# A shorter life for the activations by token, the attention residual as a matrix product, and 1,056 more columns for the attention's ring

## The chip, the cores and the metric

The kernel runs on one core of a Trainium2 chip. The metric is the device time of one execution in microseconds. All data is float32 unless a line says otherwise; a "column" below is one float32 on each of 128 partitions.

## The reference, cut to what matters

Eight residual layers with a layer norm behind each run over 4 sequences of 1,024 tokens of width 128: an attention by similarity, a binarised feed-forward, an attention among the 64 channels of each of 16 heads, a ternary feed-forward, a gated linear recurrence, four experts, a state-space layer, and a product-key mixture with the two best of 64 experts. The part that the change touches most is the third:

```python
x = _layernorm(x + _L1_attn_ref(x, ...))
# inside, for every token and head, Q, K and V of 64 values each:
scores = einsum('bshq,bshk->bshqk', Q, K)      # 64 x 64 per token and head
scores = where(triu(ones(C, C), 1), -inf, scores)
w = softmax(scores)
attn = einsum('bshqk,bshk->bshq', w, V)        # then reshaped and @ Wo
```

Each score is a product of two numbers, so the work is elementwise: exp(q*k - m) for every pair below the diagonal.

## The kernel before, in words

**Order.** The program is written out by a planner in Python. Every piece of work is a generator that yields the engine it needs next and the buffers that must be free; `Order.run` picks the step that can start first by the planner's own estimates, with ranks between steps that could start together. The planner thus fixes one order of instructions for each engine and for the DMA queue of SP; the chip then only waits on semaphores.

**Blocks and chains.** The 32 tiles of 128 tokens form 8 blocks of four tiles. Each block goes through a front (`layer0`, `layer1`), then through the channel attention tile by tile (`prepare`, `feed`, `rest`, `invert`, `close`), then through chain a (`layer3` to `layer5`), chain b (`layer6`) and chain c (`layer7`). The last block goes through the three chains as two groups of two tiles. The chains of older blocks are placed between the attention work of newer ones; when the attention has ended, only the chains of the last groups remain.

**The attention's pieces.** A unit is 64 tokens (half a tile), so there are 64 units. Each is cut into 17 pieces in a fixed order: a diagonal piece of 1,024 columns, seven pieces of 896, 768, 640, 512, 384, 256 and 128, a second diagonal piece of 1,024, and eight pieces of 1,920, 1,792, 1,664, 1,536, 1,408, 1,280, 1,152 and 1,024: 17,408 columns. A piece goes through six steps: VectorE multiplies q by k into the ring (GpSimd does so for the pieces of 896 and 1,536), GpSimd subtracts the maximum, ScalarE takes the exponential, TensorE adds up the denominator (`den`), VectorE multiplies by v, TensorE adds up the numerator (`num`). Then the piece's room is given back.

**The ring.** All pieces live in one buffer of `ERING` columns, handed out in order. A piece that does not fit between the head and the end starts again at column 0; what is left at the end stays unused in that lap. A piece can start only when the older pieces in its room have been through the numerator:

```python
def at(self, n):
    start = self.head if self.head + n <= self.size else 0
    for a, b in self.held:
        if start < b and a < start + n:
            return None
    if self.held and start < self.head:
        if any(a >= self.head for a, b in self.held):
            return None
    return start
```

After the last piece the ring is cut into pieces of 512 columns that join the buffer tags `b` and `c` of the last chains.

**Activations by token and transposed.** A block has `x` (tokens on partitions) and `xT` (features on partitions), five buffers of 512 columns for each. `x` is loaded or made in the front and kept until `layer7` writes it to DRAM (`xs`) as its first step. `close` ends a tile's attention: the product with `Wo`, an addition of `x` on VectorE (line 1053), the norm on ScalarE into `x`, a transpose into `xT`. After the front one row of `xT` (feature 96) is overwritten by ones, to carry biases; since the activations have a mean of zero over the features, that feature is minus the sum of the others. The other layers add their residual already as a product of `xT` with the identity. `layer5` adds the experts up in `x`.

Of the kernel before, what the change touches and what calls it, by code (L numbers as in the profile page):

```python
# [15 lines left out]
ALU = mybir.AluOpType  # L16
# [4 lines left out]
P = 128  # L21
NB, SEQ, D = 4, 1024, 128
NG = 8
TPG = 4
# [4 lines left out]
BIG = 3.0e38  # L29
H, C, R, S, NK = 16, 64, 4, 2, 16  # L30
SH = S * H
ERING = 8904
LUMPS = 4
EPS = 0.05
SLACK = {}
# [2 lines left out]
    "ident": P, "a0_W1": 1, "a0_b1": 1, "f0_b1": 4, "f1_lnw": 4, "f1_lnb": 4, "a2_nw": 1, "f2_b1": 16, "f2_Wu": 1,  # L38
    "f2_bu": 1, "a3_bdt": 16, "a3_Alog": 16, "f3_sup": 1, "f3_sdn": 1, "bup": 64, "bdn": 32, "rep": 32, "SL": P, "U": P,
    "ex4": P, "ex2": P, "g4": 16, "g2": 32, "su": P, "sd": P, "par": 4, "iota": LUMPS, "blk": P, "bz": 48,  # L40
    "route": 16, "beyond": R,
}
ONE = 96
LAG = {"chain_a": (0.7, 300), "chain_b": (1.6, 290), "chain_c": (2.6, 132)}
# [275 lines left out]
class Model:  # L320
# [4 lines left out]
    def __init__(self, ctx, tc, a):  # L325
        self.tc, self.nc, self.a = tc, tc.nc, a
        self.n = 0
        self.sb = ctx.enter_context(tc.tile_pool(name="sb", bufs=1))
        self.ps = ctx.enter_context(tc.tile_pool(name="ps", bufs=1, space=PSUM))
        self.dram = ctx.enter_context(tc.tile_pool(name="scratch", bufs=1, space=DRAM))  # L330
        self.order = Order(URGE, HOP)
        nc = self.nc
        self.pe, self.v, self.s, self.g, self.d = (
            (Tensor if n == "PE" else Engine)(self.order, e, n)
            for e, n in ((nc.tensor, "PE"), (nc.vector, "DVE"), (nc.scalar, "ACT"), (nc.gpsimd, "POOL"), (nc.sync, "SP"))
        )

        self.room = {
# [3 lines left out]
            "den": (1, 512), "num": (1, 512), "kvr": (2, 512), "bg": (4, 512),  # L342
        }

        self.held, self.most = 0, 2
        self.slots, self.tags, self.users = {}, {}, {}
        for tag, (n, cols) in self.room.items():
            pool = self.ps if tag in ("den", "num", "kvr", "bg") else self.sb
            self.slots[tag] = [self.keep([P, cols], tag, pool=pool) for _ in range(n)]
            for t in self.slots[tag]:  # L350
                self.tags[self.order.owner(t)] = tag, t
# [211 lines left out]
        for j in range(n):  # L563
            self.s.activation(x[:, j, :], r[:, j, :], AF.Copy, scale=rs[:, j : j + 1])

    def norm(self, g, c, r):

        x, rs = g.x, self.small([P, TPG], c + "rs")[:, : g.n]
        yield "ACT"
        self.level(x, r, rs)  # L570
        self.drop(r)
        yield from self.transpose(g.xT, [x[:, j, :] for j in range(g.n)])

    def own(self, g):

# [22 lines left out]
    def normalise(self, g, nT):  # L598
        sq = self.small([P, TPG], "sq")
        rn = self.small([P, TPG], "rn")  # L600
        yield "ACT", self.free("a")
        nrm = self.new("a", TPG, D)
        for j in range(TPG):
            self.s.activation(nrm[:, j, :], g.x[:, j, :], AF.Square, accum_out=sq[:, j : j + 1])
        yield "POOL"
        self.g.tensor_scalar_max(sq, sq, 1e-12)
        self.g.tensor_tensor(rn, sq, self.neghalf, ALU.pow)
        yield "ACT"
        for j in range(TPG):
            self.s.activation(nrm[:, j, :], g.x[:, j, :], AF.Copy, scale=rn[:, j : j + 1])  # L610
        yield from self.transpose(nT[:, (g.k % 2) * GT : (g.k % 2) * GT + GT], [nrm[:, j, :] for j in range(TPG)])
        self.drop(nrm)
        yield from self.transpose(g.xT, [g.x[:, j, :] for j in range(TPG)])

    def similar(self, nT, i, h, out):
        yield "PE", self.free("bg")
# [35 lines left out]
    def layer0(self, b):  # L652

        room = "ha" if b else "hc"
        gs = self.blocks[2 * b : 2 * b + 2]
        for g in gs:
            if g.x is None:
                yield "SP", self.free("x")
                self.load_x(g.k)
            yield "ACT", self.free("xT")  # L660
            g.xT = self.new("xT")
        yield "ACT", self.free(room)
        nT = self.new(room)
        yield from self.together(*(self.normalise(g, nT) for g in gs))
        if b == 0:
            yield from self.count(gs[0], nT)
            return nT
        yield from self.together(*(self.count(g, nT) for g in gs))
        self.drop(nT)
# [348 lines left out]
    def close(self, unit):  # L1018

        T, u = unit["T"], unit["u"]  # L1020
        g, j = divmod(T, TPG)
        yield "DVE", self.when(lambda: "a" in unit, lambda: self.order.until(unit["a"]))
        a, num, aT = unit["a"], unit["num"], self.aT
        self.v.tensor_tensor(a, num.rearrange("p h c -> p (h c)"), a, ALU.mult)
        self.drop(num)
        if unit is self.units[-1]:
            self.retire("num", "bg")
            self.most = 4

        yield "PE", self.free("bg", also=lambda: self.closed == 2 * T + u)  # L1030
        ps = self.new("bg", 4, P)
        for i in range(4):
            self.pe.transpose(ps[:, i, :], a[:, i * P : (i + 1) * P], self.ident)
        self.drop(a)
        yield "ACT"
        self.s.copy(
            aT.rearrange("p (b c) t -> p c b t", b=2)[:, :, :, 64 * u : 64 * u + 64],
            ps.rearrange("p c (b t) -> p c b t", b=2),
        )
        self.drop(ps)  # L1040
        if u == 1:
            yield "PE", self.free("bg")
            po = self.new("bg")[:, :D]
            self.bias_row(po, 1, D, first=D)
            for i in range(8):
                if i == 4:
                    yield "PE"
                self.pe.matmul(po, lhsT=aT[:, i, :], rhs=self.Wo[:, i, :], start=False, stop=(i == 7))
            self.closed += 1
            yield "DVE"  # L1050
            x = self.blocks[g].x[:, j, :]
            rs = self.small([P, 1], "crs")
            self.v.tensor_tensor(po, x, po, ALU.add)
            yield "ACT"
            self.level(x[:, None, :], po[:, None, :], rs)
            yield "PE"
            self.pe.transpose(po, x, self.ident)
            yield "ACT"
            self.s.copy(self.blocks[g].xT[:, j * P : (j + 1) * P], po)
            self.drop(po)  # L1060
            self.normed += 1
        else:
            self.closed += 1
# [83 lines left out]
    def layer4(self, g):  # L1147
        a, xT, n = self.a, g.xT, g.n
# [13 lines left out]
        q, k, f, gate = (big[:, i, :] for i in range(4))  # L1162
# [88 lines left out]
            self.pe.matmul(po[:, j, :], lhsT=og[:, j * P : (j + 1) * P], rhs=Wo, start=True, stop=False)  # L1251
            self.pe.matmul(po[:, j, :], lhsT=xT[:, j * P : (j + 1) * P], rhs=self.ident, start=False, stop=True)
        self.drop(big, og, sq, Wo)
        yield from self.norm(g, self.own(g), po)


    def layer5(self, g):
# [83 lines left out]
    def layer6(self, g):  # L1341
# [223 lines left out]
            self.pe.matmul(po[:, j, :], lhsT=drained[j // 2][:, 0, j % 2, :], rhs=Wout, start=True, stop=False)  # L1565
            self.pe.matmul(po[:, j, :], lhsT=xT[:, j * P : (j + 1) * P], rhs=self.ident, start=False, stop=True)
        self.drop(room, w, *drained, *(() if n == TPG else (dx,)))
        yield from self.norm(g, "b", po)


    def top2(self, c, pl, Q, used, expand, places, n, spread):
# [102 lines left out]

    def layer7(self, g):
        a, k, n = self.a, self.k, g.n
        xs, ys = (self.keep([n * P, D], name, pool=self.dram) for name in ("xs", "ys"))
        yield "SP"
        self.d.dma_start(xs.rearrange("(j p) d -> p j d", p=P), g.x)
        self.drop(g.x)  # L1680
        Wup = yield from self.load("c", a["f3_Wup"].rearrange("p (s e) -> p s e", e=64), 8, 64)
        yield "SP", self.free("c")
        xq = self.new("c", 4 * n, 32)
# [183 lines left out]
    def chain_a(self):  # L1867
# [14 lines left out]
        for g in self.groups:  # L1882
            b = self.blocks[g.t0 // TPG]

            yield "PE", self.when(lambda: self.done5 >= g.k - (g.k == len(self.groups) - 1))

            for k in {0: (2, 3), 1: ()}.get(g.k, range(b.k + 2, min(b.k + 3, NG)) if g.t0 % TPG == 0 else ()):
                yield from self.front(self.blocks[k])
            yield "PE", self.when(lambda: self.normed >= g.t0 + g.n, lambda: self.order.until(b.xT))
            if g.t0 % TPG == 0:  # L1890
                self.users[b.x.tensor.name] = self.users[b.xT.tensor.name] = sum(
                    o.t0 // TPG == b.k for o in self.groups
                )
            if g.n < TPG:
                self.order.split(b.x, 256)
                self.order.split(b.xT, 256)
            j = g.t0 % TPG
            g.x, g.xT = b.x[:, j : j + g.n, :], b.xT[:, j * P : (j + g.n) * P]
            self.order.spawn(one(g), "chain_a", self.order.latest)

    def chain_b(self):
# [70 lines left out]
def arrays_of(i):  # L1972
    f = {k: np.asarray(v) for k, v in i.items()}
    c = np.ascontiguousarray
# [64 lines left out]
    for n, s in (("up", "up"), ("dn", "down")):  # L2039
# [16 lines left out]
        "g4": p // 4 == np.arange(16)[None, :],  # L2056
        "g2": p % 32 == np.arange(32)[None, :],
        "beyond": (p // 32 > np.arange(R)[None, :]) * -BIG,
        "su": (p % 4 == q % 4) & (p // 4 == q // 8),
        "sd": (p % 32 == q // 4) & (p // 32 == q % 2),  # L2060
        "par": np.concatenate([p // n % 2 == np.arange(2)[None, :] for n in (4, 2)], 1) * LUMPS,
# [25 lines left out]
```

## Time and profile before

| | us |
|---|---|
| median of 3 runs (lowest, highest) | 3816.46 (3814.92, 3824.07) |
| the profiled execution, its own time | 3811.2 |
| its span, first to last instruction | 3809.4 |
| TensorE busy | 3041.4 (80%) |
| VectorE busy | 3163.6 (83%) |
| ScalarE busy | 2498.4 (66%) |
| GpSimd busy | 2815.1 (74%) |
| mean granted TensorE clock | 0.922 |

In the profile PE is TensorE's matmuls, PEld its weight loads, DVE is VectorE, ACT ScalarE, POOL GpSimd and SP the engine that issues the DMAs. All helpers share one recorded line (L60), so groups are told apart by the names of their buffers: `ringe` is the ring, `qr` and `kvr` hold queries and keys with values, `mr` the maxima, `den` and `num` are the sums in PSUM, `bg` are general PSUM banks. A group's row gives the busy time and the mean ns of one instruction, then the idle time of that engine just before these instructions and what ended it. A row of waits gives the total us, the number of waits and the longest.

### The profile page before, as it was taken

How to read it: one execution, taken by the hardware profiler on the slowest of the kernel's cores; microseconds unless marked ns; L12 is line 12 of the kernel's file. 1: busy time of each engine (PE TensorE's matmuls, PEld its weight loads, DVE VectorE, ACT ScalarE, POOL GpSimd, SP SyncE). 2: the span in 40 equal slices, each digit the busy share in tenths (PEclk: the TensorE clock that was granted, in tenths of full speed). 3: DMA queues.
4: the chain of work that ended last, by engine and by line, in shares of the span. 5: the costliest groups of instructions: out<-in, count | busy, mean ns of one | idle time of the engine just before them, and what ended most of it. 6: DMA issues, size and time to landing. Idle time of an engine off the chain costs nothing.

```text
span 3809.4 us, 130461 instructions
## 1 busy us (share of the span) xinstructions
PE 3041.4 (80%) x56496; PEld 1616.4 (42%) x56496; DVE 3163.6 (83%) x3988; ACT 2498.4 (66%) x5206; POOL 2815.1 (74%) x1320
## 2 busy tenths in 40 slices
PE   5567667877778888988888987988888887879873
PEld 2224232433334543544444543544444443446652
DVE  2888999999899889999899789899998999983321
ACT  4557565667757885777657885777666775666641
POOL 0778997899879887898878887798887997970000
PEclk8889889989999999999999998999999999989886
DMA  2332221312214334243433433343432334523564
GB/s 70 77 80 52 45 53 45 88 45 54 49 49 107 91 79 110 67 120 85 106 82 88 105 83 83 89 123 79 109 94 73 93 85 104 141 80 100 162 158 104
DMA packets 374135, 334.04 MB, mean 88 GB/s; under 512 B 196332, under 2 KB 304172, under 8 KB 373560
## 3 DMA queue, kind: packets, MB, share of 16 engines
q1 hardware_dynamic: 364216, 292.15, 30.8%
q0 software_dynamic: 9344, 33.56, 2.9%
q8 instruction: 442, 7.24, 0.8%
q14 instruction: 133, 1.09, 0.1%
HBM read 149.16 MB, written 42.21 MB: 50 GB/s over the span
## 4 chain that ended last, share of the span: by engine, by line
PE 26%; DVE 21%; ACT 13%; POOL 8%; issue 8%; DMA 3%; SPq 1%; DVEq 0%; ACTq 0%; POOLq 0%
PE bg L60 15%; DVE ringe L60 14%; POOL ringe L60 8%; ACT ringe L60 5%; PE den L60 5%; PE num L60 4%; DVE bg L60 4%; PE kvr L60 2%; ACT b L60 2%; ACT ha L60 1%; ACT x L60 1%; SPq L60 1%; ACT L60 1%; ACT t L60 1%; DVE a L60 0%
## 5 line engine op out<-in xcount | busy, mean ns | idle before, releaser
L60 POOL TENSOR_TENSOR ringe<-ringe,mr 128x1024 f32<-128x1024 f32 (+14 forms) x1088 | 2450.2, 2289 | 436.2 <-DVE ringe L60 331.7
L60 DVE TENSOR_TENSOR ringe<-ringe,kvr 128x1024 f32<-128x1024 f32 (+14 forms) x1097 | 1290.8, 1206 | 149.9 <-PE den L60 132.6
L60 ACT ACTIVATE ringe<-ringe 128x768 f32<-128x768 f32 (+14 forms) x962 | 1001.2, 1057 | 528.8 <-POOL ringe L60 525.1
L60 DVE TENSOR_TENSOR ringe<-qr,kvr 128x1024 f32<-128x1024 f32 (+12 forms) x960 | 1110.0, 1192 | 52.1 <-PE num L60 32.6
L60 PE MATMUL num<-ringe,cst 128*32 128x256 f32 (+7 forms) x8728 | 692.1, 405 | 247.4 <-DVE ringe L60 239.9
L60 PE MATMUL den<-ringe,cst 128*32 128x256 f32 (+7 forms) x8728 | 679.1, 408 | 184.7 <-ACT ringe L60 160.8
L60 PEld LDWEIGHTS num<-ringe,cst 128*32 128x32 f32 x8728 | 220.5, 112 | 566.8 <-DVE ringe L60 457.1
L60 PEld LDWEIGHTS den<-ringe,cst 128*32 128x32 f32 x8728 | 237.4, 113 | 464.4 <-ACT ringe L60 248.7
L60 POOL TENSOR_TENSOR ringe<-qr,ks 128x896 f32<-128x896 f32 (+1 forms) x128 | 287.7, 2248 | 74.7 <-PE num L60 34.7
L60 PE MATMUL bg<-xT,a 128*32 128x512 f32 (+1 forms) x1880 | 248.5, 621 | 37.4 <-DVE bg L60 11.7
L60 ACT ACTIVATE ringe<-ringe,cst 128x256 f32<-128x256 f32 x512 | 217.8, 500 | 65.0 <-POOL ringe L60 64.7
L60 DVE TENSOR_TENSOR_SCAN bg<-ends,bg 128x512 f32<-128x512 bf16 x128 | 155.3, 1218 | 37.9 <-PE bg L60 37.1
L60 PE MATMUL kvr<-wkv,xT 128*32 128x256 f32 x2048 | 150.5, 415 | 27.3 <-DVE ringe L60 26.7
L60 PE MATMUL bg<-a,ha 128*32 128x128 f32 x4608 | 154.9, 276 | 11.5 <-ACT ha L60 11.5
L60 ACT COPY b<-bg 128x512 f32<-128x512 f32 (+2 forms) x214 | 95.6, 453 | 69.7 <-PE bg L60 68.2
L60 PEld LDWEIGHTS bg<-a,ha 128*32 128x32 f32 x4608 | 123.8, 112 | 32.7 <-issue 15.1
L60 ACT ACTIVATE ha<-bg,cst 128x512 f32<-128x512 f32 (+1 forms) x155 | 100.0, 674 | 56.4 <-PE bg L60 56.1
L60 PE MATMUL bg<-xT,b 128*32 128x128 f32 (+1 forms) x3528 | 127.2, 285 | 2.7 <-ACT last L60 0.9
L60 ACT ACTIVATE b<-cst,little 128x128 f32<-128x128 f32 x392 | 124.7, 399 | 0.0
L60 PEld LDWEIGHTS bg<-xT,a 128*32 128x32 f32 x1880 | 58.4, 116 | 140.4 <-issue 60.7
L60 PEld LDWEIGHTS bg<-xT,b 128*32 128x32 f32 x3528 | 102.3, 114 | 33.4 <-issue 16.9
L60 PE MATMUL bg<-b,cst 128*32 128x512 f32 x832 | 109.8, 600 | 4.6 <-ACT b L60 4.6
(678 smaller groups left out, 4431.3 us busy)
## 6 DMA issues: line engine op xcount, KB each, us to landing
qr<-q SPq DMA_DIRECT2D x512, 128.0 KB
mr<-t SPq DMA_DIRECT2D x512, 128.0 KB
c<-in_f_Wdn SPq DMA_DIRECT2D x55, 256.0 KB
c<-tu SPq DMA_DIRECT2D x204, 64.0 KB
tu<-gt SPq DMA_DIRECT2D x25, 512.0 KB
td<-gt SPq DMA_DIRECT2D x24, 512.0 KB
c<-td SPq DMA_DIRECT2D x94, 128.0 KB
a<-in_f_W SPq DMA_DIRECT2D x36, 256.0 KB
```

The costliest lines, as they stand in the source:

```text
L60: return f(*args, **kw)
```

## The change

`x` lives only inside norms, and from `layer4`'s norm to the end of `layer5`; three buffers of 512 columns serve instead of five. `normalise` drops `x` after its transposes, `norm` takes a buffer of its own and drops it again, `layer6` writes `xs` to DRAM itself as soon as its norm is done (before, `layer7` did that first). In `close` the addition on VectorE goes; instead TensorE adds the product of `xT` with a constant `more` (the identity, with column 96 made of -1 and row 96 of 0) into the same PSUM bank ahead of the products with `Wo`, and the norm writes into a small buffer `cx`. `TensorE` matmuls of this kind are issued as four, of 32 columns of the stationary operand each. The constants grow by 128 columns, `cx` takes 128, and the ring has 9,960 columns instead of 8,904.

```diff
-ERING = 8904
+ERING = 9960
...
-    "route": 16, "beyond": R,
+    "route": 16, "beyond": R, "more": P,
...
-            "x": (5, 512), "xT": (5, 512), "a": (6, 512), "b": (12, 512), "c": (4, 512), "gt": (1, 1024), "xp": (2, 152),
+            "x": (3, 512), "xT": (5, 512), "a": (6, 512), "b": (12, 512), "c": (4, 512), "gt": (1, 1024), "xp": (2, 152),
...
-    def norm(self, g, c, r):
-
-        x, rs = g.x, self.small([P, TPG], c + "rs")[:, : g.n]
-        yield "ACT"
-        self.level(x, r, rs)
+    def norm(self, g, c, r, keep=False):
+
+        rs = self.small([P, TPG], c + "rs")[:, : g.n]
+        if g.x is None:
+            yield "ACT", self.free("x")
+            g.x = self.new("x", g.n, D)
+        else:
+            yield "ACT"
+        self.level(g.x, r, rs)
         self.drop(r)
-        yield from self.transpose(g.xT, [x[:, j, :] for j in range(g.n)])
+        yield from self.transpose(g.xT, [g.x[:, j, :] for j in range(g.n)])
+        if not keep:
+            self.drop(g.x)
+            g.x = None
...
         yield from self.transpose(g.xT, [g.x[:, j, :] for j in range(TPG)])
+        self.drop(g.x)
+        g.x = None
...
             self.bias_row(po, 1, D, first=D)
+            self.pe.matmul(
+                po, lhsT=self.blocks[g].xT[:, j * P : (j + 1) * P], rhs=self.k["more"], start=False, stop=False
+            )
             for i in range(8):
...
-            yield "DVE"
-            x = self.blocks[g].x[:, j, :]
-            rs = self.small([P, 1], "crs")
-            self.v.tensor_tensor(po, x, po, ALU.add)
+            rs, x = self.small([P, 1], "crs"), self.small([P, D], "cx", bufs=1)
             yield "ACT"
             self.level(x[:, None, :], po[:, None, :], rs)
...
-        yield from self.norm(g, self.own(g), po)
+        yield from self.norm(g, self.own(g), po, keep=True)
...
-        yield from self.norm(g, "b", po)
+        yield from self.norm(g, "b", po, keep=True)
+        yield "SP"
+        g.xs = self.keep([n * P, D], "xs", pool=self.dram)
+        self.d.dma_start(g.xs.rearrange("(j p) d -> p j d", p=P), g.x)
+        self.drop(g.x)
...
-        xs, ys = (self.keep([n * P, D], name, pool=self.dram) for name in ("xs", "ys"))
-        yield "SP"
-        self.d.dma_start(xs.rearrange("(j p) d -> p j d", p=P), g.x)
-        self.drop(g.x)
+        xs, ys = g.xs, self.keep([n * P, D], "ys", pool=self.dram)
...
+        "more": ((p == q) * 1.0 - (q == ONE)) * (p != ONE),
```

More of the change, by code (lines that the diff above doesn't have):

```diff
@@ L656, in layer0 @@
         for g in gs:
-            if g.x is None:
+            if g.k > 1:
                 yield "SP", self.free("x")
@@ L1890, in chain_a @@
             if g.t0 % TPG == 0:
-                self.users[b.x.tensor.name] = self.users[b.xT.tensor.name] = sum(
-                    o.t0 // TPG == b.k for o in self.groups
-                )
+                self.users[b.xT.tensor.name] = sum(o.t0 // TPG == b.k for o in self.groups)
             if g.n < TPG:
-                self.order.split(b.x, 256)
                 self.order.split(b.xT, 256)
             j = g.t0 % TPG
-            g.x, g.xT = b.x[:, j : j + g.n, :], b.xT[:, j * P : (j + g.n) * P]
+            g.xT = b.xT[:, j * P : (j + g.n) * P]
             self.order.spawn(one(g), "chain_a", self.order.latest)
```

## The prediction

> **What bounds the kernel now.** I read the page's busy shares first, then the busy time by stages, then the waits of VectorE and GpSimd between 500 and 3300 us, where the attention runs evenly, and last the groups by shape. In the page, DVE is near full in most slices and falls only at the end; POOL is 0 in the last four slices, because the attention has ended there:
>
> ```profile
> PE 3041.4 (80%) x56496; PEld 1616.4 (42%) x56496; DVE 3163.6 (83%) x3988; ACT 2498.4 (66%) x5206; POOL 2815.1 (74%) x1320
> ...
> DVE  2888999999899889999899789899998999983321
> ...
> POOL 0778997899879887898878887798887997970000
> ```
>
> The busy time between 500 and 3300 us (columns: PE, PEld, DVE, ACT, POOL, then clock, DMA share and GB/s):
>
> ```profile
> 500.00:3300.00 2800.00, 2338.83 (x43103) 1219.46 (x43103) 2572.86 (x3125) 1954.91 (x3942) 2339.98 (x1076) 0.95 0.34 85
> ```
>
> VectorE is busy for 2572.86/2800 = 92%, GpSimd and TensorE for 84%. VectorE idles only 2800 - 2573 = 227 us there. The waits in the same stretch say at what:
>
> ```profile
> DVE ringe L60 <- PE den L60: 98.0, 90, 4.5
> DVE ringe L60 <- PE num L60: 25.6, 21, 3.8
> ...
> POOL ringe L60 <- DVE ringe L60: 282.1, 85, 12.7
> POOL ringe L60 <- PE num L60: 55.6, 13, 11.2
> ```
>
> GpSimd's idle time is mostly lack of products from VectorE (282 us); VectorE's is the product with v waiting for the denominator (98 us). A wait of `ringe` on `num` is a full ring: 25.6 us of VectorE, 55.6 us of GpSimd. So VectorE bounds the attention, from about 100 to 3422 us (the last numerator), and a full ring is the smaller of its troubles. Behind it lies a tail of 390 us in the chains of the last groups, with VectorE far from full.
>
> **The change part by part.**
>
> *The addition in `close`.* Its row, and the nearest rows for what takes its place:
>
> ```profile
> L60 DVE TENSOR_TENSOR bg<-x,bg 128x128 f32<-128x128 f32 x31 | 8.9, 286 | 7.8 <-PE bg L60 7.7
> ...
> L60 PE MATMUL bg<-cst,xT 128*32 128x128 f32 x944 | 48.1, 276 | 0.0
> ```
>
> 32 additions (31 in this row, one under `kvr`) of 0.286 us are 9.2 us of VectorE, and in front of them it stood 7.7 us waiting for the products with `Wo`. With the addition gone both go from VectorE's queue. The busy part counts in full, since VectorE is the full engine. Of the wait I take half, 3.9 us: the other half returns, since VectorE then only comes earlier to the next piece, whose denominator it waits for. Sum -13.1, bounds 0 (TensorE's and ScalarE's chain sets the end, and VectorE's time is only redistributed) and -16.9.
>
> TensorE gets 32 x 4 = 128 matmuls of exactly the form of the second row, which is the residual of the other layers. 48.1/944 = 0.051 us each in a stream, 6.5 us in all; if each group of four shows its 0.276 us alone, 8.8 us. TensorE is 84% busy, and the products with `Wo` of the same bank are queued behind them: I take +1 for the denominators that come later by them, bounds 0 and +8.8.
>
> The Trainium skill ("TensorE: Matmul & The Clock Gate", Back-to-back issue gap) speaks against this part: it gives about 81 ns for each matmul of 128 columns in a sustained stream of weight loads and matmuls, which would make 128 x 0.081 = 10.4 us (an estimate), more than the addition's 9.2. The row shows 51 ns, so the row decides; with the page's figure the sum below would be worse by at most 4 us.
>
> The step from addition to norm vanishes from the last tile's path too: one 0.3 us instruction against about 0.2 us of matmuls, so nothing.
>
> *The ring.* The positions follow from the code and the fixed order of pieces, whatever the timing. With 8,904 columns one lap holds the last piece of a unit (1,024), the next unit's first nine and its 1,920: 8,576. The next lap holds 1,792 to 1,152: 8,832. With 9,960 a lap holds 1,664 to 1,024 and the next unit's first 1,024: 9,088; the following 896 would end at 9,984, 24 columns too far. So it wraps, and the next lap takes 896 to 1,792: 8,320, and again 1,664 would end at 9,984. Both sizes make two laps for each unit of 17,408 columns. **The 1,056 columns hold no more pieces on average; they only move the two wraps.** Working out which older piece each piece waits for:
> - the first 1,024 of a unit waits for the numerator of 1,792 instead of 1,664, one piece older, hence earlier. 768, 384 and the second 1,024 gain likewise, but they rarely wait.
> - 1,152 waits for 1,792 of its own unit, five pieces back, instead of 1,920, six back. Its room in flight ahead of it falls from 7,680 to 5,888 columns; the least for any piece before is 6,400.
> - the other twelve, among them 1,536, for which GpSimd waits, and 1,408 and 1,280, keep their piece.
>
> ```profile
> L60 DVE TENSOR_TENSOR ringe<-qr,kvr 128x1024 f32<-128x1024 f32 x192 | 232.0, 1212 | 27.9 <-ACT ks L60 16.1 <-PE num L60 8.6 <-DMA qr<-q 3.0
> ...
> L60 DVE TENSOR_TENSOR ringe<-qr,kvr 128x1408 f32<-128x1408 f32 x64 | 103.2, 1612 | 10.9 <-PE num L60 10.9
> ...
> L60 DVE TENSOR_TENSOR ringe<-qr,kvr 128x1152 f32<-128x1152 f32 x64 | 86.1, 1346 | 0.0
> ```
>
> What can go is the 8.6 us in the row of 1,024 (the 10.9 of 1,408 stays): -8.6, bounds 0 and -8.6. GpSimd's 55.6 us stay. What comes is a wait in the row of 1,152, which has none now. From the timeline I compared, in each unit, the start of that product with the end of the numerator of 1,792. In 15 of 63 units it now starts before that end, by 32.6 us in sum. Eleven of them are short by 1.7 us or less (9.9 us together), and VectorE has another product ready to go ahead. The four others are short by 4.3, 7.8, 5.4 and 5.2 us. One of these (the row merges the products of 1,280 and 1,152; the second starts at 1289.8, and `num` with 448 columns is the piece of 1,792, ending at 1294.1):
>
> ```profile
> 1288.39 2.75 DVE L60 TENSOR_TENSOR ringe<-qr,kvr 128x1280 f32<-128x1280 f32 x2 [0.33 <-PE num L60]
> 1291.06 2.01 DVE L60 TENSOR_TENSOR ringe<-ringe,kvr 128x1792 f32<-128x1792 f32 x1
> ...
> 1293.15 0.94 PE L60 MATMUL num<-ringe,cst 128*32 128x448 f32 x8
> ```
>
> The product with v of 1,792 that releases it stands directly behind it, and other work follows, so part of the delay is only an exchange of order: I take 1.5 us for each of the four, +6, bounds 0 and +32.6. Behind a waiting product of 1,152 in VectorE's queue stand products with v, and GpSimd waits for its subtraction. Where the cover of other VectorE work fails, it is the whole 32.6.
>
> *Life of `x`, and `xs`.* Three buffers look fewer, but `layer0` holds two only while no `layer5` runs (chain a does fronts and layers in turn), `layer5` holds one, `layer6` one. Starts of fronts stay bound by the five `xT`, which are dropped later in `layer7` than `x` was. The write of `xs` moves from the head of `layer7` to the end of `layer6` in SP's queue, nine DMAs of the same size; past whatever SP issues between, its stalls behind ScalarE's norm (47.8 us over 7 waits now) may grow or shrink, with weights and replicas behind them, but VectorE waits for those replicas only 3.0 us. In the last group the write starts at 3704.5 and the first gathered tables reach the core at 3749, so its round trip is covered. Taken as 0, bounds -3 and +3. The tail has two more pieces of 512 columns (19 instead of 17): 0, bounds -5 and 0, since no buffer shows as a wait on the tail's chain. The constant adds 64 KB to a load of 607.5 KB: nothing.
>
> *Sum:* -13.1 + 1 - 8.6 + 6 = -14.7. Against the profiled execution 3811.2 becomes 3796.5; it lies 5.3 us under the median, so 3816.5 - 14.7 = 3802.
>
> *What no row shows* is the new order. The planner decides again at every step, and the trace shows how much order matters: from one unit's last numerator to the next's, with the same work, it takes 40 to 72 us. I bound it by a tenth of VectorE's 227 idle us, 23 us either way.
>
> **The rivals.**
> - *No change (3814):* VectorE's 13 us only turn into waits for `den` (98 us show that the loop through GpSimd, ScalarE and TensorE is nearly as tight), and the ring's two moved waits cancel: -8.6 + 6 = -2.6. For it speaks GpSimd's 84%.
> - *Slower, by the wrap (3845):* the wait of 1,152 on the piece five back becomes the ring's narrowest place, in every unit. Priced at the full 32.6, with TensorE's full 8.8, VectorE's 13.1 gained and nothing from the 1,024 row: 32.6 + 8.8 - 13.1 = 28.3, so 3816.5 + 28.3 = 3845. It decides over the forecast where the wait at 1,152 passes some 21 us. For it: GpSimd has no product to subtract meanwhile, and a hungry GpSimd already idles 282 us. Against: the shortage is under 1.7 us in eleven of fifteen cases.
> - *The ring does give room (3766):* the planner keeps more in flight after all, all waits on `num` of ringe go (25.6 of VectorE) and VectorE's full 16.9 are won, with some 8 of GpSimd's 55.6. Against it the two laps above; I leave it 8 in 100.
>
> **How the numbers follow.** A measurement of this kernel tells some 0.3%, 11 us, from no change. The forecast holds 0.34, the ring that gives room 0.08: faster 0.42. No change has 0.27. Slower by the wrap, or by an order of that size, 0.31. The likeliest is the forecast, 3802; its own range is 3779 to 3816 or so (bounds of the terms and part of the order's 23). The full range takes in the rivals on both sides: 3765 to 3845.
>
> **What would show it.** Right: the row of `bg<-x,bg` is gone, `bg<-cst,xT` has about 128 more; VectorE's busy time is 9 us lower; the 1,024 row has almost no `PE num` wait; the 1,152 row has one, of 5 to 15 us; the 1,408 and 1,536 rows wait about as before; the last numerator ends some 15 us earlier and the tail stays near 390. Wrong: over 20 us in the 1,152 row, or a last numerator that does not move (then VectorE was not the bound), or a tail that changes by over 10 us (then the buffers or the order of the last groups matter).

## The result and the profile after

The changed kernel takes 3833.95 us (median of 6 runs, 3831.14 to 3838.0) against 3815.83 us before: ratio 1.0045, 95% interval 1.0033 to 1.0057. The forecast was 3802, faster; it was slower by 17 us (0.45%). (Ratios here and below are worked out from the single runs, with a 95% interval, so one can differ a little from the quotient of the medians beside it.)

The profiled execution has a span of 3829.4 us, 20.0 more than before. From the timeline, the last numerator of the attention ends at 3453.2 us instead of 3421.8, and the tail takes 376.2 us instead of 387.6: the attention lost 31.4 us and the tail won 11.4. The page's busy shares and slices:

```profile
PE 3065.0 (80%) x56752; PEld 1629.3 (43%) x56752; DVE 3157.3 (82%) x3956; ACT 2499.7 (65%) x5206; POOL 2811.9 (73%) x1320
...
DVE  2888988999989899899998889899898989884321
...
POOL 0778996998879886898788877798777987880010
```

VectorE has 32 instructions and 6.3 us of work less. TensorE has 256 more records for 128 matmuls: each of these float32 matmuls is two in the trace. Busy time between 500 and 3300 us, and the waits in that stretch (columns as before):

```profile
500.00:3300.00 2800.00, 2340.00 (x42831) 1218.46 (x42827) 2541.48 (x3068) 1940.57 (x3915) 2309.17 (x1062) 0.94 0.34 85
```

```profile
DVE ringe L60 <- PE den L60: 108.7, 93, 4.9
DVE ringe L60 <- PE num L60: 37.9, 28, 4.9
...
POOL ringe L60 <- DVE ringe L60: 322.2, 93, 18.0
POOL ringe L60 <- PE num L60: 45.5, 12, 12.3
```

In the same 2800 us VectorE did 31.4 us less (2541.5 against 2572.9), GpSimd 30.8 us less. Nothing became long; there is more waiting in between, most of it GpSimd's for products (282 to 322). By shape, the products into the ring. First one row of before, then three of after:

```profile
L60 DVE TENSOR_TENSOR ringe<-qr,kvr 128x1792 f32<-128x1792 f32 x64 | 128.8, 2012 | 1.5 <-PE num L60 1.3
```

```profile
L60 DVE TENSOR_TENSOR ringe<-qr,kvr 128x1024 f32<-128x1024 f32 x192 | 231.8, 1216 | 23.7 <-ACT ks L60 23.4
...
L60 DVE TENSOR_TENSOR ringe<-qr,kvr 128x1792 f32<-128x1792 f32 x64 | 129.3, 2020 | 14.5 <-PE num L60 14.5
...
L60 DVE TENSOR_TENSOR ringe<-qr,kvr 128x1152 f32<-128x1152 f32 x64 | 86.4, 1350 | 10.7 <-PE num L60 10.7
```

The wraps moved as worked out from the code: the 1,024 row has lost its wait on `num`, and 1,152, which had none, waits 10.7 us. But 1,792, whose piece to wait for did not change, went from 1.3 to 14.5 us, as much again. So the picture was open to three readings: the moved wrap costs the time (theory 1); the planner dealt out another order and it is a worse one (theory 2; below, O stands for it); the product or the short life of `x` costs it (theory 3; P stands for the product alone).

### The profile page after: what moved, and what is told of

Its sections match the earlier page's. It is cut to its first block, busy times and chain, and to the rows that moved or that the text cites. A ratio compares the mean times of both kernels' runs of the same rounds, so it can differ in the third digit from the quotient of the medians.

```text
span 3829.4 us, 130895 instructions
## 1 busy us (share of the span) xinstructions
PE 3065.0 (80%) x56752; PEld 1629.3 (43%) x56752; DVE 3157.3 (82%) x3956; ACT 2499.7 (65%) x5206; POOL 2811.9 (73%) x1320
## 5 line engine op out<-in xcount | busy, mean ns | idle before, releaser
L60 ACT ACTIVATE ringe<-ringe 128x256 f32<-128x256 f32 (+14 forms) x962 | 1000.8, 1057 | 533.8 <-POOL ringe L60 530.2
L60 PE MATMUL den<-ringe,cst 128*32 128x32 f32 (+7 forms) x8720 | 682.4, 412 | 200.2 <-ACT ringe L60 171.1
L60 DVE TENSOR_TENSOR_SCAN bg<-ends,bg 128x512 f32<-128x512 bf16 x128 | 155.7, 1221 | 40.4 <-PE bg L60 36.4
L60 POOL DMA_INDIRECT gt<-in_f_tup,dlumps x16 | 15.7, 980 | 136.6 <-ACT dep L60 112.8
```

Of the source, the lines that this page charges most:

```text
L60: return f(*args, **kw)
```

## The experiments

**The parts, each planned anew.** Four kernels: the change with the old ring, the change with 24 more columns, and two that put one part alone into the kernel before.

e1, the change with the ring of before:

```diff
-ERING = 9960
+ERING = 8904
```

> The changed kernel with the ring back at 8,904 columns; all else as changed. Theory 1 (the moved wrap costs the time): the piece of 1,152 waits six pieces back again, so the loss of 17 us goes, and the addition's gain remains: 3800 to 3815, no numerator wait in the 1,152 row, 5 to 12 us again in the 1,024 row, last numerator at 3400 to 3420. Theory 2 (any edit makes the planner deal the instructions anew, and this deal is a worse one): anything from 3795 to 3840, with no relation to the ring's rows. Theory 3 (the short life of x, with the early write of xs in SP's queue, or the product, costs the time): 3830 to 3840, as changed.

Measured 3852.66 us, ratio 1.0086 (1.0072 to 1.0100), last numerator at 3461.5. Undoing the ring made it slower, and the time lies above the ranges of all three theories. The rows behaved as theory 1 had it (1,152 without a wait, 8.1 us on `num` at 1,024), but the time did the opposite. Theory 1 is not the main cause.

e2, 24 columns more, in the room of one small buffer:

```diff
-ERING = 9960
+ERING = 9984
...
-        l = self.small([64, 64], c + "lg")[:Q]
+        l = self.small([64, 64], c + "lg", bufs=1)[:Q]
```

> The changed kernel with 24 more columns in the ring, 9,984, where 896 and 1,664 still fit before the wrap; the room comes from one small buffer of 64 columns that is no longer doubled. By the positions, laps per unit fall from 2.00 to 1.83 and no piece waits for a later one than in the kernel before. Theory 1: faster than the changed kernel by 17 us or more: 3785 to 3815, waits of ringe on num below half of the changed kernel's. Theory 2: anything from 3795 to 3840. Theory 3: 3825 to 3840.

3831.22 us, ratio 1.0037 (1.0023 to 1.0050), last numerator at 3435.2. VectorE's waits of `ringe` on `num` fell to 15.8 us between 500 and 3300, and the attention ended 18 us sooner than in the changed kernel, yet the time gained almost nothing: the tail took it back (391.5 us). A second profile of the same kernel (e11 below) has its last numerator at 3442.6, so 7 us between two single profiles need no cause.

e3, the kernel before with the wraps of the changed one:

```diff
-ERING = 8904
+ERING = 9088
...
-        self.held, self.head, self.past = deque(), 0, []
+        self.held, self.head, self.past = deque(), 8064, []
```

> The kernel before with a ring of 9,088 columns whose first piece starts at column 8,064: from then on every piece waits for exactly the piece that it waits for in the changed kernel (1,152 five pieces back). Nothing else is changed. Theory 1: slower than before by 15 to 30 us (3830 to 3845), a wait of about 10 us in the 1,152 row, none in the 1,024 row. Theory 2: 3795 to 3840. Theory 3: as before, 3810 to 3820.

3844.05 us, ratio 1.0066 (1.0053 to 1.0079): what theory 1 wanted. But its 1,152 row waits only 4.7 us for `num` and the 1,792 row 4.4, and between 500 and 3300 us VectorE's waits at the ring even fell, from 25.6 us before to 19.5; that does not add up to 27 us.

e4, the kernel before with the product alone:

```diff
...
             self.bias_row(po, 1, D, first=D)
+            self.pe.matmul(
+                po, lhsT=self.blocks[g].xT[:, j * P : (j + 1) * P], rhs=self.k["more"], start=False, stop=False
+            )
...
-            yield "DVE"
             x = self.blocks[g].x[:, j, :]
             rs = self.small([P, 1], "crs")
-            self.v.tensor_tensor(po, x, po, ALU.add)
```

> The kernel before with the attention's residual as a product from xT (constant of 128 columns added), x kept as before and ring at 8,904. Theory 1: faster than before by the 13 us of the addition: 3798 to 3810. Theory 2: 3795 to 3840. Theory 3, if the product is what costs: 3825 to 3835; if the life of x is: 3800 to 3816.

3852.16 us, ratio 1.0087 (1.0074 to 1.0100), last numerator at 3464.2: 35 us more, again above all the ranges, for an exchange that takes 9 us from the full engine. Either 128 matmuls cost far more than their row, or the order does.

**Work and order held apart.** The planner only knows what is noted to it. So one can note one thing and execute another. In e5 the planner goes on noting the addition, and the order stays that of the kernel before (in the trace, GpSimd's and ScalarE's instructions follow each other exactly as before, and VectorE's differ by the 32 additions alone):

```diff
...
             self.bias_row(po, 1, D, first=D)
+            xt = self.blocks[g].xT[:, j * P : (j + 1) * P]
+            for c in range(0, P, 32):
+                self.pe.real.matmul(po[c : c + 32], lhsT=xt[:, c : c + 32], rhs=self.k["more"], start=False, stop=False)
...
-            self.v.tensor_tensor(po, x, po, ALU.add)
+            self.order.note("DVE", "tensor_tensor", (po, x, po, ALU.add), {})
```

> The kernel before with the product executed in place of the addition, while the planner goes on noting the addition: every engine's order of instructions stays that of the kernel before, only 128 matmuls stand in TensorE's queue and 32 additions are gone from VectorE's. Theory P (the product itself costs the 35 us of the run with the product alone, by TensorE's time): 3845 to 3855. Theory O (the 35 us are the new order that the planner deals out once the step is gone): 3803 to 3818, the direct gain of my sum or a part of it.

3815.65 us beside 3819.01 before, ratio 0.9987 (0.9977 to 0.9997); e17 is the same kernel again, with about as many runs:

> A repeat in five rounds of the kernel before with the product executed in place of the addition and the old order kept: 0.1 to 0.3% faster than before, 3805 to 3814 where the kernel before shows 3815.

3814.66 beside 3813.8, ratio 1.0000 (0.9991 to 1.0010), last numerator at 3420.8 (before 3421.8). Theory P falls. The gain of 5 us that e5 shows did not come again in e17: with the order kept, the exchange is worth between nothing and 5 us, and no cost of it shows. The profile of e17, first the page's line, then the waits between 500 and 3300 us:

```profile
PE 3049.0 (80%) x56752; PEld 1628.1 (43%) x56752; DVE 3156.1 (83%) x3956; ACT 2498.4 (66%) x5206; POOL 2815.0 (74%) x1320
```

```profile
POOL ringe L60 <- DVE ringe L60: 292.9, 90, 12.9
DVE ringe L60 <- PE den L60: 114.6, 102, 5.6
POOL ringe L60 <- PE num L60: 48.6, 12, 10.8
DVE ringe L60 <- PE num L60: 27.6, 22, 3.8
```

VectorE has 7.5 us less to do, and the wait for the denominator rose from 98.0 to 114.6 us, 16.6 more (114.5 in e5): VectorE comes earlier to the same denominators and waits there. That is the mechanism of the rival "no change".

e6 is the counterpart, the order of e4 with the addition executed (the edit against e4):

```diff
-            self.pe.matmul(
-                po, lhsT=self.blocks[g].xT[:, j * P : (j + 1) * P], rhs=self.k["more"], start=False, stop=False
-            )
+            xt = self.blocks[g].xT[:, j * P : (j + 1) * P]
+            for c in range(0, P, 32):
+                kw = dict(lhsT=xt[:, c : c + 32], rhs=self.k["more"])
+                self.order.note("PE", "matmul", (po[c : c + 32],), kw)
...
+            self.v.real.tensor_tensor(po, x, po, ALU.add)
```

> The counterpart: the planner notes the product, so that the order is that of the run with the product alone, but the addition on VectorE is executed. Theory P: 3810 to 3820. Theory O: 3845 to 3865.

3864.22 us, ratio 1.0113 (1.0095 to 1.0131). The work of the kernel before in the order of e4 loses 45 us. So order is what costs. By the medians e4 lies 12 us under e6, which has the same order, but the two ratios' intervals overlap and the last numerators lie at 3464.2 and 3463.3: a gain of the exchange in the attention does not show in this order either.

**New orders of unchanged work.** Three shifts of the planner's own numbers, with the kernel before:

```diff
-EPS = 0.05
+EPS = 0.06
```

> The kernel before with no change of its work: the planner's window for steps that could start together is 0.06 us instead of 0.05, so it deals out another order. Theory O in its strong form (the kernel before has an order that was chosen among many, and nearly any other one is slower): 3825 to 3860. If the order matters little: 3812 to 3820.

```diff
-HOP = {"close": 0.2, "prepare": 0.2, "chain_a": 0.5, "chain_b": 0.5, "chain_c": 0.5, "rest": 0.1, "feed": 0.1}
+HOP = {"close": 0.2, "prepare": 0.2, "chain_a": 0.5, "chain_b": 0.5, "chain_c": 0.5, "rest": 0.12, "feed": 0.1}
```

> As the run before, another way to a new order with the same work: the planner's hop for the steps of the attention's pieces is 0.12 us instead of 0.1. Theory O in its strong form: 3825 to 3860. If the order matters little: 3812 to 3820.

```diff
-        }.get(op, 0.075 + 1.045e-3 * n)
+        }.get(op, 0.077 + 1.045e-3 * n)
```

> The kernel before with the planner's fixed cost of a VectorE instruction at 0.077 us instead of 0.075: a third order of the same work. If the order of the kernel before is a chosen one: 3825 to 3870. If 3829 and 3869 were exceptions: 3812 to 3820.

The ratios were 1.0016 (1.0005 to 1.0027), 1.0120 (1.0097 to 1.0143) and 1.0092 (1.0067 to 1.0117). Not a byte of the work differs, and all three are slower, by up to 50 us. In the attention they lose what the changed kernel loses, 30 to 35 us: the last numerator lies at 3452.2, 3452.1 and 3457.2. Their tails take 374.6, 406.9 and 394.1 us, before 387.6, so much of the difference between the three is made behind the attention. The stretch from 500 to 3300 of the second (e8) shows the same loss of VectorE's and GpSimd's work as after the change:

```profile
500.00:3300.00 2800.00, 2337.57 (x42560) 1216.04 (x42556) 2544.74 (x3093) 1934.51 (x3916) 2310.07 (x1063) 0.95 0.34 84
```

**The same shifts on the changed kernel** (e10 with the window, e13 with the hop; edits as in e7 and e8):

> The changed kernel with the planner's window at 0.06 us: same work, another order. If orders scatter as they did for the kernel before (3829 and 3869 beside 3817), this lands anywhere in 3815 to 3870, and the changed kernel's 3834 is one draw of such a spread. If the change costs by itself, it lies above the kernel before under the same shift of the window, 3829, by some 17 us: about 3846.

> The changed kernel with the planner's hop at 0.12 us; the kernel before gave 3869 under the same shift. If the change itself costs some 17 us, this lies near 3886. If times scatter with the order whatever the edit, it lies anywhere in 3815 to 3870.

1.0091 (1.0068 to 1.0114) and 1.0076 (1.0050 to 1.0102). With the change as it is, three orders give 1.0045, 1.0091 and 1.0076, mean 1.0071; three shifted orders of the kernel before give mean 1.0076. The window shift was worse with the change (1.0091 against 1.0016), the hop shift better (1.0076 against 1.0120). A cost or gain of the change itself does not show above that spread; with three orders on each side, between 0.16% and 1.2%, one of the size of the 0.45% could hide in it.

**The ring of 9,984 under three more orders** (e11 is the kernel of e2 run once more, in spite of its label; it took 3835.38 us):

> A repeat of the ring of 9,984 on this chip, one look, to stand beside the two shifted planners: 3825 to 3835.

> The changed kernel with a ring of 9,984 and the planner's hop at 0.12 us: another order. With the kernel before the same shift gave 3869. If room in the ring makes the time less dependent on the order, this lies well under that: 3815 to 3840. If not, anywhere up to 3870.

> The changed kernel with a ring of 9,984 and the planner's window at 0.06 us; the other two orders of this ring gave 3831 and 3837. If room makes the time depend less on the order: 3820 to 3840. If not, up to 3870.

> The ring of 9,984 under the same shift of the fixed cost: 3820 to 3840 if the room narrows the spread, up to 3870 if not.

Ratios 1.0048 (1.0029 to 1.0068), 1.0100 (1.0075 to 1.0124) and 1.0045 (1.0023 to 1.0067), with e2 a mean of 1.0058. That is a little under the two other means, but e14 alone is as slow as any; that room narrows the spread is not shown.

**Room in the ring with the order kept.** e9 has the changed kernel's order, planned with 9,960, while the pieces lie in a ring of 9,984:

```diff
+        self.real = 0
...
         self.head = start + n
+        start = self.real if self.real + n <= 9984 else 0
+        self.real = start + n
         return self.ap[:, start : start + n]
...
-        self.ering = Ring(self.keep([P, ERING], "ringe"), ERING)
+        self.ering = Ring(self.keep([P, 9984], "ringe"), ERING)
...
```

> The changed kernel with exactly its order of instructions (planned with a ring of 9,960), while the pieces really lie in a ring of 9,984, where 1,152 waits for 1,920 six pieces back and no piece for a later one. Only the waits for room change. If the moved wrap costs something by itself, the 10.7 us in the 1,152 row go and the time falls by 5 to 15 us to 3820 to 3829. If the waits at the ring only stand in for others, it stays within 4 us of the changed kernel, 3830 to 3838.

3828.79 us, ratio 1.0029 (1.0017 to 1.0040) where the changed kernel has 1.0045, last numerator 3445.9 instead of 3453.2. Its waits and the row of 1,152:

```profile
POOL ringe L60 <- DVE ringe L60: 331.5, 85, 18.0
DVE ringe L60 <- PE den L60: 118.7, 104, 5.3
POOL ringe L60 <- PE num L60: 21.7, 6, 12.3
DVE ringe L60 <- PE num L60: 15.4, 14, 2.9
```

```profile
L60 DVE TENSOR_TENSOR ringe<-qr,kvr 128x1152 f32<-128x1152 f32 x64 | 86.3, 1349 | 0.0
```

The 10.7 us are gone, with 22.5 us of VectorE's waits at the ring in all and 23.8 of GpSimd's; the last numerator comes 7.3 us earlier, no more than the two profiles of e2's kernel differ, and the intervals of the two ratios overlap. The other waits grew (`den` from 108.7 to 118.7, GpSimd's for products from 322.2 to 331.5). So at this order the moved wrap's direct price is some 6 us by the ratios (an estimate that reaches down to nothing), and of VectorE's 22.5 us about two thirds or more came back as other waits.

e18 does the same with e1's order, planned for 8,904 (the tail alone is dealt out anew, since the ring's room is cut up otherwise there):

> The changed kernel with the order planned for a ring of 8,904 through the whole attention (only the tail is dealt out anew), while the pieces really lie in a ring of 9,984 and wait for older pieces. With the true ring of 8,904 the last numerator ended at 3461.5 us. If room helps only by fewer waits on the chip, it ends 5 to 12 us earlier, at 3450 to 3456, and the time is 3838 to 3850. If a bigger ring helps by letting the planner deal out another order, it stays within 4 us of 3461.

The last numerator ended at 3459.1 instead of 3461.5, 2.4 us, though VectorE's waits on `num` fell from 36.4 to 20.0 us. So no worth of the columns to a fixed order shows. The time fell to 3831.7 us, ratio 1.0050 (1.0034 to 1.0065), because its new tail took 372.4 us instead of 392.2. The tail, too, depends on the order that it gets.

No version is shown to beat the kernel before: e5 and e17, which have its order, are its equal.

## Why the prediction was wrong, point by point

- **The step that failed is "What no row shows".** I gave the new order 23 us either way, from a tenth of VectorE's idle time, and centred it on zero. The runs have thirteen other orders through the attention (e6 shares that of e4, e9 that of the changed kernel, e18 that of e1), with very different edits or none, and all of them are slower, by 0.16% to 1.2% (6 to 46 us of 3816). In all thirteen the last numerator comes later, at 3435 to 3474 us against 3421 to 3422 in the three profiles of the old order (before, e5, e17); the tails, 372 to 407 us, scatter to both sides of the old order's 388 to 393. The spread was under-sized by half and, above all, it is not centred: the order of the kernel before lies at the fast end of those that the planner dealt out here. Nothing in one profile of it could show that it did; the 40 to 72 us from unit to unit showed that order matters, and I used it only as a width. The 0.31 for "slower" did name an order of that size, but the sum that I forecast had it at nothing.
- **The addition.** VectorE's work fell about as counted (9.2 expected; 6.3 less in the changed kernel, 7.5 in e17). "The busy part counts in full, since VectorE is the full engine" is wrong: where I had -13.1 + 1, the exchange with the order kept gained 0 (e17) to 5 us (e5), and 16.6 us more waiting for `den` took up the rest, about what the row of the additions had held (8.9 busy and 7.7 waiting). VectorE, busy 92% of the time in a fixed order of a loop through four engines, did not by itself set the pace of that loop. The lower bound that I named for the term, 0, is what e17 shows.
- **The product.** Mis-sized by two: 128 matmuls are 256 records. The products have a row of their own in e5, 12.5 us for 248 of them, where I had 6.5 for all (1.0 on the path):

```profile
L1047 PE MATMUL bg<-cst,xT 128*32 128x128 f32 x248 | 12.5, 272 | 0.0
```

 At 50 ns a record the price that I read from the other residuals holds, but a matmul of the program is two records, some 101 ns. The 81 ns of the Trainium skill ("TensorE: Matmul & The Clock Gate", Back-to-back issue gap) is neither of the two. On the path no cost of it shows (e17).
- **The ring.** The geometry held: two laps either way, the wait gone at 1,024 and come at 1,152, here 10.7 us where I had allowed 5 to 15 in the row. But rows whose piece to wait for did not change moved as much: 1,792 from 1.3 to 14.5, 1,408, which I expected to stay, from 10.9 to 5.9. I had put the two at -8.6 and +6 on the path; e9 gives some 6 us, not clear of nothing, for having the moved wrap instead of a ring with room. The rival that priced the moved wrap at 32.6 us was right about the sign of the result, but by luck: with the old wraps (e1) the changed kernel is slower still.
- **`x`, `xs` and the tail.** No wait shows that three buffers are too few: between 500 and 3300 us all of ScalarE's waits in front of writing `x` or `cx` fell together from 27.5 to 19.1 us, those for TensorE in front of `x` from 11.2 to 8.7. SP's stalls behind the norm grew with the earlier write of `xs`, but between 500 and 3300 us the engines' waits for DMAs fell, from 26.9 to 8.9 us over VectorE, GpSimd, ScalarE and TensorE with its weight loads. SP's own waits, before and after:

```profile
SPq L60 <- ACT x L60: 47.8, 7, 21.9
```

```profile
SPq L60 <- ACT x L60: 110.9, 7, 33.6
```

 I expected a tail that stays near 390; it fell by 11.4 us. e18 shows that a new order of the tail alone can move it by 20, so I do not put this down to the two pieces of 512 columns.

What stays open: by which property the order of the kernel before is faster. The lost time is spread over the attention as short waits of VectorE and GpSimd, not at one place; the lag behind the kernel before, unit by unit, goes from 16 us ahead (27th unit) to 31 behind at the end, up and down. Whether the short life of `x` has a price of its own was not held apart from the order; no wait shows one, and the means over three orders leave it under the spread.

The granted clock was not held apart either. The six runs of the changed kernel had mean granted TensorE clocks of 0.916 to 0.920, 0.918 on average; the kernel before, in the five sessions of the experiments, had 0.920 to 0.922. Runs of one and the same kernel are longer where their mean clock is lower, by 1.4 us for each 0.001 in a fit over all kernels run three times or more (0.9 to 2.5 in the single sessions of the kernel before). By that fit the lower clock would go with 4 to 7 of the 17 us (an estimate; up to 12 at the steepest of the sessions); whether the order lowers it is not shown. It is not all that the orders cost: e1 and e3, at 0.921 and 0.920 beside 0.921 for the kernel before, lost 33 and 25 us.

## What to carry to other kernels

Where a planner deals out one fixed order, any edit that it can see is two edits: the work, and a new draw of the order. Cost the first from rows, but ask for the second how the present order compares with its neighbours, by shifting a planner's number that changes no work; here that spread was 0.2 to 1.2% on the slow side, up to three times the sum forecast for the edit's own terms (46 us against 14.7). And to learn what a part is worth, note the old instruction to the planner and execute the new one.

A ring's room is set by where its pieces wrap, not by its columns: 1,056 more left the laps at two for a unit, and 24 beyond them made them 1.83, though no gain in time clear of the noise came even of that (e9). Work out the laps before giving room.

## What the runs showed of the hardware that was not expected

A float32 matmul with 32 columns of the stationary operand appears as two records, of about 50 ns each in a stream (12.5 us for 248). And VectorE, busy for 92% of a stretch, lost 7.5 us of work in e17 with no change of the time beyond 0.1%: its waits for TensorE's denominators grew by 16.6 us.
